# Attention stage: the previous image's last products with v ahead of an image's first scores, the first image's k moved by ScalarE, another order in the last half image

## The chip, the cores and the metric

The kernel runs on one core of a Trainium2 chip. The metric is the device time of one execution in microseconds (us), as the median of several runs. The core has a matrix engine (TensorE, PE in the profile), VectorE (DVE), ScalarE (ACT), GpSimd (POOL) and SyncE (SP), which work side by side and wait for one another by semaphores. SP, ACT and POOL also issue DMAs. Matrix products land in PSUM, everything else is in SBUF.

## The reference

The input x is an array of 8 images with 384 channels and 32 x 32 pixels, in float32. Four layers follow one another, each of the form x + f(GroupNorm(x)).

- Layer 0 is the one that is changed here. For each of q, k and v: a depthwise 3x3 convolution, a batch norm (mean and variance over all images and pixels), gelu, and a 384 x 384 product over the channels. Then attention over the 1024 pixels of an image with 8 heads of 48 channels, an output projection w_out, and a batch norm.
- Layer 1 is a mixture of 4 experts (the best 2 by a gate), layer 2 a 7x7 depthwise convolution, layer 3 three branches with convolutions and small MLPs that are fused.

```
y = dwconv3x3(x)                       # for q, k and v, each with own weights
y = gelu(batch_norm(y))                # statistics over batch and pixels
q, k, v = pw @ y                       # 384 x 384, per image
att = softmax(q.T @ k / sqrt(48)) @ v  # per image and head, 1024 x 1024
out = batch_norm(w_out @ att)
```

## The kernel before, in words

**Convolution stage.** The 384 channels are three tiles `ct` of 128. A loop runs over 36 groups n = (ct, v, u): channel tile, which of q, k, v (0, 1, 2), and a quarter u of the rows. A group is a set of banded matmuls (L373) into a PSUM tile `ps` (2 buffers). Its weights come by a DMA on ACT's queue (L319) and are spread by `spread0(n)` into `wx` (3 buffers), one half by ACT (L327), one by POOL (L328), two groups ahead. ACT copies `ps` into `o` (L406), a tile for four groups with 2 buffers. When a set of four is complete, `results()` on DVE transposes an image's share (L342), takes batch norm statistics (L164) and SP stores it to `raw[v][b]` in HBM (L344); these calls are spread over the next four groups, and the last set's follow after the loop. When all of q or k is there, `coefs0(v)` makes the batch norm's scale and shift: DVE (L230, L158), a power on POOL (L159), and DVE again (L232 to L234). `y0` loads image 0's q or k back (on SP), and `gelu0(v)` applies scale, shift and gelu on ACT (L224). The order on PE, ACT and DVE is the written order (`manual_schedule(engines=ORDERED)`); POOL and SP are ordered by a scheduler.

**Attention stage**, `attention(False)`. The same three engines run in written order. The list `todo` has (b, h, pair, g): image, half of its query pixels, pair of heads (4 pairs), and half of its key pixels. So an image has 16 steps, numbered j. For each step

- `scores` makes four score tiles of 128 x 1024 (L597), and ACT takes exp of each (`e`, L604, 8 buffers);
- `attend` multiplies the e of the step before with v (L616) into a tile `av` (2 buffers in PSUM). Row sums come out of the same product, as vT has columns of ones;
- after the second g, `norm` shuffles the sums (L630), takes the reciprocal (L632) and multiplies (L634, or L638 for the fourth pair), and checks the sums against overflow (L644, L647).

The first three pairs write rows of `att` directly; the fourth goes to `att3` and from there by three POOL DMAs (L640) into every fourth row of `att`. `project_out(b, h)` then makes z = w_out @ att (L655), and DVE copies z and takes moments (L659 to L663); POOL stores z (L668).

At j = 0 of an image come `project_k` and `project_q` (L505), both through `spread`: for each of three tiles a product into PSUM, an ACT affine that writes all 128 rows (L224), and 32-row moves by DVE that gather the fourth pair (L523; for q L525 with a factor). Then follow scores, the attend of the previous image's last step, and `project_v` (L550):

```
es = scores(*t)
complete = attend(*last) if last else None
if j == 0:
    project_v(b)
```

The PSUM pool `sc` has three tiles of two banks (`two_banks`), which k, q, v, scores and project_out all take in turn. For the first image, `begun` is true: gelu of k and q is done by `gelu0`, and that of v (`activate(b, 2)`) follows project_q.

**After the last step**: `attend`, `norm`, the check's minimum (`ok`, L712, L713), one matmul with ones that adds it up (L717), `shift_needed` (L718), and `project_out(7, 1)`. `shift_needed` is loaded as a value (L726), and an `If` (L727) would repeat attention with a shift of the maximum; it is not taken in these runs. The next stage begins with `bn_coefs(zst, ...)` on DVE (L230).

Of the kernel before, what the change touches and what calls it, by code (L numbers as in the profile page):

```python
# [11 lines left out]
FP = mybir.dt.float32  # L12
# [6 lines left out]
P = 128  # L19
# [71 lines left out]
def conv_mixer_kernel(ctx: ExitStack, tc: tile.TileContext, a: dict, out: bass.AP):  # L91
# [171 lines left out]
    with (  # L263
        tc.tile_pool(name="cw", bufs=1) as cw,
        tc.tile_pool(name="cxa", bufs=1) as cxa,
        tc.tile_pool(name="co", bufs=2, reuse_waits="tile") as co,
        tc.manual_schedule(engines=ORDERED),
    ):
        bn_gb = load(cw, "bn_gb", nc.scalar)
        stats = cw.tile([P, 9, 2 * B, 6], FP, name="stats")  # L270
# [19 lines left out]
        with tc.tile_pool(name="cy", bufs=3, reuse_waits="tile") as cy, tc.tile_pool(  # L290
# [72 lines left out]
            for n, (ct, v, u) in enumerate(groups):  # L363
                if u == 0:

                    o = co.tile([P, B, H, 32], FP, tag="o", name="o")
                w = weights0.pop(n).rearrange("p r t w -> p r (t w)")
                ps = cps.tile([P, 4, 2, B, H], FP, tag="ps", name="ps")
                for cc in range(2):
                    for k in range(3):  # L370
                        for e, d, i in product(range(2), repeat=3):
                            r = slice(64 * i, 64 * i + 64)
                            nc.tensor.matmul(  # L373
                                ps[64 * d : 64 * d + 64, 2 * i + e, cc],
                                lhsT=w[r, 12 * cc + 6 * e + 3 * d + k, :],
                                rhs=xt0s[ct][r, 16 * d + 8 * e + 2 * u + cc, :, k : k + H],
                                start=k == 0, stop=k == 2,
                            )
# [27 lines left out]
                nc.scalar.copy(  # L406
                    o.rearrange("p b h (i c) -> p i c (b h)", i=4)[:, :, 2 * u : 2 * u + 2],
                    ps.rearrange("p i c b h -> p i c (b h)"),
                )
# [26 lines left out]
    def attention(shifted):  # L436
# [3 lines left out]
        with tc.tile_pool(name="aw", reuse_waits="tile", bufs=1) as aw, tc.tile_pool(  # L440
# [68 lines left out]
                        )  # L509
                return ps.rearrange("p h n -> p (h n)")  # L510

            def spread(w, y, o, own):


                for t in range(NC):
                    ps = project(w, t, y)
                    to = [[(0, None)], [(32, 1), (64, 2)], [(96, None)]][t]
                    affine(o[:, t, :], ps, own[:, 0:1] if own is not None else 1.0, 0.0)
                    moves = [(o[64:96, t, :], 32, 2)]
                    moves += [(o[p : p + 32, NP - 1, :], 64, i) for p, i in to]  # L520
                    for d, p, i in moves:
                        if own is None or i is None:
                            nc.vector.tensor_copy(d, ps[p : p + 32, :])  # L523
                        else:
                            nc.vector.tensor_scalar(  # L525
                                d, ps[p : p + 32, :], own[p : p + 32, i : i + 1], None, ALU.mult
                            )

            def project_k(b):
                kT = kTs[b] = ay.tile([P, NP, N], FP, tag="kT", name="kT", bufs=1)  # L530
                if not shifted:
                    return spread(pw_k, ys[b][1], kT, None)
                for pair in range(NP):
                    affine(kT[:, pair, :], project(pw_k, pair, ys[b][1]), 1.0, ones_row)

# [69 lines left out]
                    es.append(e)  # L605
                return es

            def attend(b, h, pair, g, es):

                if g == 0:  # L610
                    attend.av = avp.tile([P, HF], FP, tag="av", name="av")
# [1 line left out]
                for e, m in zip(es, range(g * GM, (g + 1) * GM)):  # L613
                    for s in range(2):
# [2 lines left out]
                            av[64 * s : 64 * s + 64, :], lhsT=vT[:, m, c0 : c0 + 64],  # L617
                            rhs=e[:, s, :], start=m == 0, stop=m == N // P - 1,
                        )
                if g == NG - 1:  # L620
                    return lambda: norm(b, h, pair, av)

            def norm(b, h, pair, av):

                if pair == 0:
# [5 lines left out]
                inv = ay.tile([P, HF], FP, tag="inv", name="inv")  # L631
                nc.vector.reciprocal(inv, sm)  # L632
                if pair < NC:
                    nc.vector.tensor_mul(atts[b, h][:, pair, :], av, inv)  # L634
                else:

                    att3 = ay.tile([P, HF], FP, tag="att3", name="att3")
                    nc.vector.tensor_mul(att3, av, inv)  # L638
                    for t in range(NC):
                        nc.gpsimd.dma_start(out=atts[b, h][3::4, t, :], in_=att3[t::4, :])  # L640
                if not shifted:

                    i = (b * 2 + h) * NP + pair
                    nc.vector.scalar_tensor_tensor(  # L644
# [1 line left out]
                    )  # L646
                    nc.vector.tensor_reduce(chk[:, i : i + 1], inv, AX.X, ALU.min)  # L647

            def project_out(b, h):
                att, x, k = atts.pop((b, h)), xs.pop((b, h)), 2 * b + h  # L650
                z = ay.tile([P, NC, HF], FP, tag="z", name="z", bufs=1 if shifted else 2)
                for oc in range(NC):
                    ps = two_banks()[:, 0, :]
                    for t in range(NC):
                        nc.tensor.matmul(  # L655
                            ps, lhsT=w_out[:, t, oc * P : (oc + 1) * P], rhs=att[:, t, :],
                            start=t == 0, stop=t == NC - 1,
                        )
                    nc.vector.tensor_copy(z[:, oc, :], ps)  # L659
                    nc.vector.bn_stats(zst[:, oc, k, :], z[:, oc, :])  # L660
                    nc.vector.bn_aggr(mvz[:, :, oc, k], zst[:, oc, k, :])
                    nc.vector.bn_aggr(mvxh[:, :, oc, k], xst[:, oc, k, :])
                    nc.vector.scalar_tensor_tensor(  # L663
                        out=x[:, oc, :], in0=z[:, oc, :], scalar=mvz[:, 0, oc, k : k + 1],
                        in1=x[:, oc, :], op0=ALU.subtract, op1=ALU.mult,
                        accum_out=zx[:, oc, k : k + 1],
                    )
                nc.gpsimd.dma_start(out=zraw[b][:, :, h * HF : (h + 1) * HF], in_=z)  # L668
# [41 lines left out]
            if not shifted:  # L710
                ok = small.tile([P, 1], FP, tag="ok1", name="ok1")
# [6 lines left out]
                nc.vector.tensor_scalar(shift_needed, ps[:1, :1], P - 0.5, None, ALU.is_lt)  # L718
            project_out(B - 1, 1)

    with tc.manual_schedule(engines=ORDERED):
        attention(False)
# [1054 lines left out]
def lay_out(inp):  # L1777
# [37 lines left out]
        o[f"pw_{v}"] = tiles_b(w.reshape(C, NC, P))  # L1815
    o["pw_v"] = tiles_b(f["L0_conv_pw_v"].T)
    w = f["L0_conv_w_out"].T[:, ORDER_A].reshape(NP, 32, 3, C)
    w = np.concatenate([w[:NC], w[NC].swapaxes(0, 1)[:, :, None]], 2)
    o["w_out"] = np.moveaxis(w.reshape(NC, P, C), 0, 1)

# [96 lines left out]
```

## Time and profile before

| what | value |
| --- | --- |
| median of 3 runs | 3377.09 us (3377.02 to 3389.05) |
| the profiled execution: its time, its span | 3390.1 us, 3388.4 us |
| mean granted TensorE clock | 0.972 |
| PE busy | 3156.8 us, 93% of the span |
| DVE, ACT, POOL busy | 1609.1, 1333.1, 238.0 us |
| convolution stage, last groups | 229 to 290 us: PE busy 44.63 of 61 |
| attention, first image's start | 290 to 360 us: PE busy 59.32 of 70 |
| attention, steady | 360 to 1744 us: PE busy 1365.27 of 1384 |
| attention, end | 1744 to 1772 us: PE busy 18.06 of 28 |
| into the next layer | 1772 to 1795 us: PE busy 7.57 of 23 |

A row of the timeline has the start in us, the busy time in us, the engine and line, the operation with out<-in, the tile's shape, the number of instructions that it joins, and in brackets the idle time of the engine before it with what ended it. Rows that are joined (x36) have the busy time of all. A row of the chain has the start, its length and what it was; "issue" is time in which nothing that the profile shows was waited for. A matmul in float32 appears as two PE instructions for most tiles here (L655 has nine products and x18).

### The profile page before, as it was taken

How to read it: one execution, taken by the hardware profiler on the slowest of the kernel's cores; microseconds unless marked ns; L12 is line 12 of the kernel's file. 1: busy time of each engine (PE TensorE's matmuls, PEld its weight loads, DVE VectorE, ACT ScalarE, POOL GpSimd, SP SyncE). 2: the span in 40 equal slices, each digit the busy share in tenths (PEclk: the TensorE clock that was granted, in tenths of full speed). 3: DMA queues.
4: the chain of work that ended last, by engine and by line, in shares of the span. 5: the costliest groups of instructions: out<-in, count | busy, mean ns of one | idle time of the engine just before them, and what ended most of it. 6: DMA issues, size and time to landing. Idle time of an engine off the chain costs nothing.

```text
span 3388.4 us, 40142 instructions
## 1 busy us (share of the span) xinstructions
PE 3156.8 (93%) x16784; PEld 1467.1 (43%) x16784; DVE 1609.1 (47%) x2199; ACT 1333.1 (39%) x1375; POOL 238.0 (7%) x398
## 2 busy tenths in 40 slices
PE   5887999999999999999988999999999998985989
PEld 4763333343434343433323444444444444654544
DVE  6997344444444444444453554343343342356164
ACT  4874453535354444445424302121121111556520
POOL 3321000000000000000000000000000000110300
PEclk9998999999999999999998999999999998997989
DMA  5886011010101110110017313121121111666766
GB/s 211 287 290 242 20 40 58 28 70 22 66 32 59 40 59 22 56 42 19 21 38 266 101 50 99 47 79 42 56 79 42 44 39 35 238 211 220 229 203 200
DMA packets 97862, 339.06 MB, mean 100 GB/s; under 512 B 14440, under 2 KB 17088, under 8 KB 93320
## 3 DMA queue, kind: packets, MB, share of 16 engines
q1 hardware_dynamic: 73672, 266.95, 23.4%
q10 hardware_dynamic: 13776, 36.90, 3.5%
q0 software_dynamic: 10224, 32.56, 2.8%
q8 instruction: 134, 2.20, 0.3%
q14 instruction: 56, 0.46, 0.0%
HBM read 237.18 MB, written 102.32 MB: 100 GB/s over the span
## 4 chain that ended last, share of the span: by engine, by line
PE 68%; issue 10%; DVE 9%; DMA 7%; ACT 4%; POOL 1%; ACTq 0%; SPq 0%; POOLq 0%; DVEq 0%
PE av L616 14%; PE sc L597 13%; PE ph L815 9%; PE y L1028 9%; PE sc L505 7%; PE sc L550 4%; PE sc L655 4%; DVE stats L164 2%; DVE y L342 2%; PE ps L1369 2%; DMA cb<-cfmem 1%; DMA w<-in_w 1%; PE po L1747 1%; PE po L1750 1%; PE po L1758 1%
## 5 line engine op out<-in xcount | busy, mean ns | idle before, releaser
L604 ACT ACTIVATE e<-sc 128x1024 f32<-128x1024 f32 x512 | 484.2, 1030 | 583.0 <-PE sc L597 582.8
L1028 PE MATMUL y<-hs,w 128*128 128x512 f32 x1152 | 521.5, 594 | 10.2 <-DVE hs L1013 10.2
L815 PE MATMUL ph<-xn,w 128*128 128x512 f32 x1152 | 526.7, 596 | 2.0 <-ACT xn L224 2.0
L597 PE MATMUL sc<-qT,kT 64*128 64x512 f32 x2048 | 481.8, 607 | 22.1 <-DVE qT L523 15.4
L616 PE MATMUL av<-e,vT 128*64 128x512 f32 x2048 | 468.9, 600 | 0.0
L819 ACT ACTIVATE hs<-ph,b 128x512 f32<-128x512 f32 x192 | 131.6, 685 | 642.3 <-PE ph L815 634.6
L1028 PEld LDWEIGHTS y<-hs,w 128*128 128x128 f32 x1152 | 217.1, 190 | 286.4 <-issue 258.6
L815 PEld LDWEIGHTS ph<-xn,w 128*128 128x128 f32 x1152 | 216.9, 191 | 270.3 <-issue 260.7
L597 PEld LDWEIGHTS sc<-qT,kT 64*128 64x128 f32 x2048 | 186.5, 186 | 309.9 <-issue 232.0
L1013 DVE TENSOR_TENSOR hs<-hs,cb 128x512 f32<-128x512 f32 x192 | 130.0, 686 | 376.1 <-ACT hs L819 370.0
L616 PEld LDWEIGHTS av<-e,vT 128*64 128x64 f32 x2048 | 135.9, 137 | 318.6 <-issue 318.6
L505 PE MATMUL sc<-y,pw 128*128 128x512 f32 x576 | 253.9, 602 | 13.6 <-issue 7.3
L373 PE MATMUL ps<-xt,wx 64*64 64x256 f32 x3456 | 199.8, 389 | 47.1 <-DVE xt L309 19.8
L632 DVE RECIPROCAL inv<-sm 128x512 f32<-128x512 f32 x64 | 214.6, 3353 | 2.2
L630 DVE LOAD_MASK_SELECT sm<-av x64 | 0.9, 14 | 417.1 <-PE av L616 417.1
L373 PEld LDWEIGHTS ps<-xt,wx 64*64 64x64 f32 x3456 | 153.1, 138 | 92.7 <-issue 44.6
L1369 PE MATMUL ps<-xt,wx 64*64 64x256 f32 x2688 | 161.1, 399 | 21.5 <-ACT wx L1116 16.5
L505 PEld LDWEIGHTS sc<-y,pw 128*128 128x128 f32 x576 | 110.3, 193 | 156.6 <-issue 147.1
L1018 DVE SCALAR_TENSOR_TENSOR r<-cb,b,r 128x512 f32<-128x512 f32 x192 | 134.2, 745 | 73.0 <-DMA cb<-cfmem 69.8
L406 ACT COPY o<-ps 128x2048 f32<-128x2048 f32 x36 | 135.1, 3759 | 55.1 <-PE ps L373 33.1
L1116 ACT ACTIVATE wx<-w,parity 128x448 f32<-128x448 f32 (+2 forms) x192 | 108.3, 617 | 105.4 <-POOL w L1103 31.7
L1369 PEld LDWEIGHTS ps<-xt,wx 64*64 64x64 f32 x2688 | 106.5, 140 | 75.0 <-ACT wx L1116 19.7
(299 smaller groups left out, 2895.7 us busy)
## 6 DMA issues: line engine op xcount, KB each, us to landing
raw<-y SPq DMA_DIRECT2D x72, 512.0 KB
y<-raw SPq DMA_DIRECT2D x24, 1536.0 KB
xr<-in_x SPq DMA_DIRECT2D x42, 512.0 KB
cb<-cfmem SPq DMA_DIRECT2D x64, 256.0 KB
w<-in_w ACTq DMA_DIRECT2D x36, 384.0 KB
xn<-in_x SPq DMA_DIRECT2D x24, 512.0 KB
x<-in_x SPq DMA_DIRECT2D x16, 768.0 KB
z<-z POOLq DMA_DIRECT2D x16, 768.0 KB, 4.3
```

Source lines behind the costliest of these rows:

```text
L373: nc.tensor.matmul(ps[64 * d : 64 * d + 64, 2 * i + e, cc], lhsT=w[r, 12 * cc + 6 * e + 3 * d + k, :], rhs=xt0s[ct][r, 16 * d + 8 * e + 2 ...
L406: nc.scalar.copy(o.rearrange("p b h (i c) -> p i c (b h)", i=4)[:, :, 2 * u : 2 * u + 2], ps.rearrange("p i c b h -> p i c (b h)"),)
L505: nc.tensor.matmul(ps[:, h, :], lhsT=w[:, ct, pair, :], rhs=y[:, ct, h * HF : (h + 1) * HF], start=ct == 0, stop=ct == NC - 1,)
L550: nc.tensor.matmul(ps[:, m, :C], lhsT=y[:, ct, (m0 + m) * P : (m0 + m + 1) * P], rhs=pw_v[:, ct, :], start=ct == 0, stop=ct == NC - 1,)
L597: nc.tensor.matmul(sc[:, s, :], lhsT=kTs[b][r, pair, m * P : (m + 1) * P], rhs=qTs[b][r, pair, h * HF : (h + 1) * HF], start=True, stop=True,)
L604: nc.scalar.activation(e, sc, AF.Exp, scale=1.0 if shifted else HD**-0.5)
L616: nc.tensor.matmul(av[64 * s : 64 * s + 64, :], lhsT=vT[:, m, c0 : c0 + 64], rhs=e[:, s, :], start=m == 0, stop=m == N // P - 1,)
L632: nc.vector.reciprocal(inv, sm)
L655: nc.tensor.matmul(ps, lhsT=w_out[:, t, oc * P : (oc + 1) * P], rhs=att[:, t, :], start=t == 0, stop=t == NC - 1,)
L815: nc.tensor.matmul(ph, lhsT=w1[:, e, ct, dc * P : (dc + 1) * P], rhs=xn[:, ct, :], start=ct == 0, stop=ct == NC - 1,)
L1028: nc.tensor.matmul(py[oc], lhsT=w2[:, e, dc, oc * P : (oc + 1) * P], rhs=hs, start=k == 0, stop=k == len(TODO) - 1,)
L1369: nc.tensor.matmul(ps[64 * d : 64 * d + 64, 2 * i + e, c % 2], lhsT=w[r, d * K7 + k, :], rhs=xts[ct][r, 16 * d + 8 * e + c, :, k : k + H], ...
```

## The change

1. In the convolution stage POOL too runs in written order.
2. The load of `y0` moves from u = 3 to u = 1; `coefs0(v - 1)` and `gelu0` stand ahead of the group's copy of `ps` instead of behind it.
3. For image 0, the 32-row moves of k are ACT copies instead of DVE copies (`spread(..., act=b == 0)`), seven of them.
4. At j = 0 of images 1 to 7, `attend` of the previous image's last step stands ahead of the scores, so that the order on PE is k, q, attend, scores, v. For image 0, `project_v` stands ahead of the first scores: k, q, v, scores.
5. In the last half image (7, h = 1) the pairs go in the order 3, 0, 1, 2. `att3` of this half is not scattered into `att`; the output projection uses it as a fourth tile, with its own weights `w_last` (four tiles, prepared by the host's layout, loaded by SP at step 1 of image 7 into the buffer of `y0`). After the last attend, the products for att3, pair 0 and pair 1 stand on PE, then those for pair 2, which wait for `norm`. ACT copies z, DVE takes the moments from PSUM, and the check follows the last norm's product. The matmul with ones writes to an `av` tile.

```diff
-        tc.manual_schedule(engines=ORDERED),
+        tc.manual_schedule(engines=ORDERED | {mybir.EngineType.Pool}),
...
+                if ct == NC - 1 and v > 0 and u == 1:
+                    y0 = pp0.tile([P, NC, N], FP, tag=f"y{v - 1}", name="y0")
+                    nc.sync.dma_start(out=y0, in_=raw[v - 1][0])
+                    ys0[v - 1] = y0
+                if ct == NC - 1 and v > 0 and u == 3:
+                    coefs0(v - 1)
+                if m == 8 and u in (1, 3):
+                    gelu0(u // 2)
                 nc.scalar.copy(
...
                 if u == 3:
                     last, last_o = (ct, v), o
-                    if ct == NC - 1 and v > 0:
-                        coefs0(v - 1)
-                        y0 = pp0.tile([P, NC, N], FP, tag=f"y{v - 1}", name="y0")
-                        nc.sync.dma_start(out=y0, in_=raw[v - 1][0])
-                        ys0[v - 1] = y0
-                if m == 8 and u in (1, 3):
-                    gelu0(u // 2)
...
-                        if own is None or i is None:
+                        if act:
+                            nc.scalar.copy(d, ps[p : p + 32, :])
+                        elif own is None or i is None:
...
-                    return spread(pw_k, ys[b][1], kT, None)
+                    return spread(pw_k, ys[b][1], kT, None, b == 0)
...
-                    for t in range(NC):
-                        nc.gpsimd.dma_start(out=atts[b, h][3::4, t, :], in_=att3[t::4, :])
-                if not shifted:
+                    if (b, h) == (B - 1, 1):
+                        atts[NC] = att3
+                    else:
+                        for t in range(NC):
+                            nc.gpsimd.dma_start(out=atts[b, h][3::4, t, :], in_=att3[t::4, :])
...
+            def project_tile(ps, att, oc, t, w):
+                nc.tensor.matmul(
+                    ps, lhsT=w[:, t, oc * P : (oc + 1) * P], rhs=att,
+                    start=t == (0 if w is w_out else NC), stop=t == NC - 1,
+                )
...
             todo = [
                 (b, h, pair, g)
-                for b in range(B) for h in range(2) for pair in range(NP) for g in range(NG)
+                for b in range(B) for h in range(2)
+                for pair in (range(NP) if (b, h) != (B - 1, 1) else (NP - 1, *range(NC)))
+                for g in range(NG)
             ]
...
+                complete = None
+                if j == 0:
+                    if last:
+                        complete = attend(*last)
+                    if begun:
+                        project_v(b)
                 es = scores(*t)
-                complete = attend(*last) if last else None
+                if j > 0:
+                    complete = attend(*last)
+                if (b, j) == (B - 1, 1):
+
+                    y = pp0.tile([P, NC, N], FP, tag="y0", name="w_last", bufs=1)
+                    w_last = y.rearrange("p c n -> p (c n)")[:, : NP * C]
+                    w_last = w_last.rearrange("p (t c) -> p t c", c=C)
+                    nc.sync.dma_start(out=w_last, in_=a["w_last"])
                 if j == 0:
-                    project_v(b)
+                    if not begun:
+                        project_v(b)
...
-            attend(*last)()
-
+            b, h = B - 1, 1
+            k = 2 * b + h
+            av_last = attend(*last, keep=True)
+            att, x = atts.pop((b, h)), xs.pop((b, h))
+            z = ay.tile([P, NC, HF], FP, tag="z", name="z", bufs=1 if shifted else 2)
+            outs = [two_banks()[:, 0, :] for _ in range(NC)]
+            att3 = atts.pop(NC)
+            for t in (NC, *range(NC - 1)):
+                for oc in range(NC):
+                    project_tile(outs[oc], att3 if t == NC else att[:, t, :], oc, t, w_last)
+            for oc in range(NC):
+                half_moments_x(oc, k)
+            check_sums = norm(b, h, NC - 1, av_last, check=False, att=att)
+            for oc in range(NC):
+                project_tile(outs[oc], att[:, NC - 1, :], oc, NC - 1, w_last)
+                nc.scalar.copy(z[:, oc, :], outs[oc])
+            nc.gpsimd.dma_start(out=zraw[b][:, :, h * HF : (h + 1) * HF], in_=z)
             if not shifted:
+                check_sums()
                 ok = small.tile([P, 1], FP, tag="ok1", name="ok1")
...
-                ps = two_banks()[:, 0, :]
+                ps = avp.tile([P, HF], FP, tag="av", name="av")
...
-            project_out(B - 1, 1)
+            for oc in range(NC):
+                moments(outs[oc], x, oc, k, of_x=False)
+                if oc == 0 and not shifted:
+                    nc.vector.tensor_scalar(shift_needed, ps[:1, :1], P - 0.5, None, ALU.is_lt)
```

`moments` holds what `project_out` did for each third (statistics of z and the product with x), and `half_moments_x` the one aggregate of x in it.

More of the change, by code (lines that the diff above doesn't have):

```diff
@@ L510, in project, with spread @@
                 return ps.rearrange("p h n -> p (h n)")
-            def spread(w, y, o, own):
+            def spread(w, y, o, own, act=False):
                 for t in range(NC):
@@ L606, in scores, with attend @@
                 return es
-            def attend(b, h, pair, g, es):
+            def attend(b, h, pair, g, es, keep=False):
                 if g == 0:
@@ L619, in attend, with norm @@
                         )
+                if keep:
+                    return av
                 if g == NG - 1:
                     return lambda: norm(b, h, pair, av)
-            def norm(b, h, pair, av):
-                if pair == 0:
+            def norm(b, h, pair, av, check=True, att=None):
+                if att is None and (b, h) not in xs:
                     x = xs[b, h] = ay.tile([P, NC, HF], FP, tag="x", name="x", bufs=1)
@@ L633, in norm @@
                 if pair < NC:
-                    nc.vector.tensor_mul(atts[b, h][:, pair, :], av, inv)
+                    att = atts[b, h] if att is None else att
+                    nc.vector.tensor_mul(att[:, pair, :], av, inv)
                 else:
@@ L638, in norm, with check_sums @@
                     nc.vector.tensor_mul(att3, av, inv)
-                    for t in range(NC):
-                        nc.gpsimd.dma_start(out=atts[b, h][3::4, t, :], in_=att3[t::4, :])
-                if not shifted:
+                    if (b, h) == (B - 1, 1):
[3 more added lines that the diff above has]
+                            nc.gpsimd.dma_start(out=atts[b, h][3::4, t, :], in_=att3[t::4, :])
+                def check_sums():
                     i = (b * 2 + h) * NP + pair
@@ L647, in norm @@
                     nc.vector.tensor_reduce(chk[:, i : i + 1], inv, AX.X, ALU.min)
+                if not shifted:
+                    if not check:
+                        return check_sums
+                    check_sums()
             def project_out(b, h):
@@ L654, in project_out, with half_moments_x, moments @@
                     for t in range(NC):
[L655 to L658, printed above, removed]
+                        project_tile(ps, att[:, t, :], oc, t, w_out)
                     nc.vector.tensor_copy(z[:, oc, :], ps)
[L660 to L668, printed above, removed]
+                    moments(z[:, oc, :], x, oc, k)
+                nc.gpsimd.dma_start(out=zraw[b][:, :, h * HF : (h + 1) * HF], in_=z)
+            def project_tile(ps, att, oc, t, w):
[3 more added lines that the diff above has]
+                )
+            def half_moments_x(oc, k):
+                nc.vector.bn_aggr(mvxh[:, :, oc, k], xst[:, oc, k, :])
+            def moments(z, x, oc, k, of_x=True):
+                nc.vector.bn_stats(zst[:, oc, k, :], z)
+                nc.vector.bn_aggr(mvz[:, :, oc, k], zst[:, oc, k, :])
+                if of_x:
+                    half_moments_x(oc, k)
+                nc.vector.scalar_tensor_tensor(
+                    out=x[:, oc, :], in0=z, scalar=mvz[:, 0, oc, k : k + 1],
+                    in1=x[:, oc, :], op0=ALU.subtract, op1=ALU.mult,
+                    accum_out=zx[:, oc, k : k + 1],
+                )
             todo = [
                 (b, h, pair, g)
-                for b in range(B) for h in range(2) for pair in range(NP) for g in range(NG)
+                for b in range(B) for h in range(2)
+                for pair in (range(NP) if (b, h) != (B - 1, 1) else (NP - 1, *range(NC)))
+                for g in range(NG)
             ]
@@ L707, in attention @@
                     project_out(b, 0)
-            attend(*last)()
+            b, h = B - 1, 1
[9 more added lines that the diff above has]
+            for oc in range(NC):
+                half_moments_x(oc, k)
+            check_sums = norm(b, h, NC - 1, av_last, check=False, att=att)
[3 more added lines that the diff above has]
+            nc.gpsimd.dma_start(out=zraw[b][:, :, h * HF : (h + 1) * HF], in_=z)
             if not shifted:
+                check_sums()
                 ok = small.tile([P, 1], FP, tag="ok1", name="ok1")
@@ L715, in attention @@
                 nc.gpsimd.memset(ones_col, 1.0)
-                ps = two_banks()[:, 0, :]
+                ps = avp.tile([P, HF], FP, tag="av", name="av")
                 nc.tensor.matmul(ps[:1, :1], lhsT=ok, rhs=ones_col, start=True, stop=True)
-                nc.vector.tensor_scalar(shift_needed, ps[:1, :1], P - 0.5, None, ALU.is_lt)
-            project_out(B - 1, 1)
+            for oc in range(NC):
+                moments(outs[oc], x, oc, k, of_x=False)
+                if oc == 0 and not shifted:
+                    nc.vector.tensor_scalar(shift_needed, ps[:1, :1], P - 0.5, None, ALU.is_lt)
     with tc.manual_schedule(engines=ORDERED):
@@ L1817, in lay_out @@
     w = f["L0_conv_w_out"].T[:, ORDER_A].reshape(NP, 32, 3, C)
+    wl = np.pad(w, ((0, 0), (0, 0), (0, 1), (0, 0)))
+    o["w_last"] = np.moveaxis(wl.reshape(NP, P, C), 0, 1)
     w = np.concatenate([w[:NC], w[NC].swapaxes(0, 1)[:, :, None]], 2)
```

## The prediction

> **What bounds the kernel now.** I read the page's chain that ended last, then that chain in order of time, then the timeline at the joints of the attention stage. The page says who sets the end:
>
> ```profile
> PE 68%; issue 10%; DVE 9%; DMA 7%; ACT 4%; POOL 1%; ACTq 0%; SPq 0%; POOLq 0%; DVEq 0%
> ```
>
> TensorE carries the end, so an edit is worth what it takes out of PE's waits. In the windows view PE is busy 1365.27 us of the 1384 from 360 to 1744 us: inside attention little can be won, and it has to come from the joints. The chain in order of time (start us, us, what) shows one, the start of image 2:
>
> ```profile
> 659.00 31.11 PE sc L505 x72
> ...
> 690.14 1.12 ACT qT L224
> ...
> 691.28 1.28 DVE qT L525
> ...
> 692.58 1.24 DVE qT L523
> ...
> 693.95 1.99 PE sc L597 x8
> 695.93 3.58 PE av L616 x16
> 699.52 15.68 PE sc L550 x48
> ```
>
> The products for k and q end at 690.11. Two score tiles run at once; the third needs the PSUM tile that q's last moves (ACT, DVE, DVE) still read, so PE waits until 693.95. Only then come the previous image's last products with v (L616) and project_v (L550). From 690.11 to 699.52 is 9.41 us. The steady pattern does the same work in 3.63 + 3.58 = 7.21 us:
>
> ```profile
> 358.81 3.63 PE sc L597 x16
> 362.45 3.58 PE av L616 x16
> ```
>
> Images 1 and 3 lose more. The timeline of image 3 (start, us, engine and line; in brackets idle before) has, after the same wait,
>
> ```profile
> 875.27 2.46 PE L597 MATMUL sc<-qT,kT 64*128 64x512 f32 x8 [1.93 <-DVE qT L523]
> 877.66 4.83 PE L616 MATMUL av<-e,vT 128*64 128x512 f32 x16
> ```
>
> where image 2 has 1.99 and 3.65. From the first score (871.36) to project_v (882.42) it takes 11.06 us; the granted clock of the window around it is 0.97, of image 2's 1.00.
>
> At the first image DVE and ACT hold PE. The timeline around 285 to 315 us:
>
> ```profile
> 283.47 0.16 DVE L234 TENSOR_TENSOR bn_t<-bn_gb,bn_t 128x3 f32<-128x3 f32 x1
> 288.77 3.48 ACT L224 ACTIVATE y<-y,bn_t,bn_s 128x1024 f32<-128x1024 f32 x3
> 288.99 1.25 DVE L342 STREAM_TRANSPOSE y<-o 128x1024 f32<-128x1024 f32 x1 [5.36 <-ACT o L406]
> 307.61 2.86 ACT L224 ACTIVATE kT<-sc 128x1024 f32<-128x1024 f32 x3 [15.36 <-DVE y L342]
> 311.96 6.17 DVE L523 COPY kT<-sc 32x1024 f32<-32x1024 f32 x5
> 314.51 18.55 PE L505 MATMUL sc<-y,pw 128*128 128x512 f32 x36 [7.31 <-issue]
> ```
>
> k's products are done at 307.2 and wait: ACT may write kT only after DVE's last transpose (306.27 + 1.23 = 307.50), and DVE's k moves come after its statistics, two of them (2.45 us) before the first PSUM tile is free and q can start at 314.51. At the other end of the stage:
>
> ```profile
> 1751.87 3.35 DVE L632 RECIPROCAL inv<-sm 128x512 f32<-128x512 f32 x1
> 1758.38 10.81 PE L655 MATMUL sc<-att,w_out 128*128 128x512 f32 x18 [0.21 <-DMA att<-att]
> 1770.22 0.74 POOL L668 DMA_DIRECT2D z<-z  x1 [12.17 <-DVE z L659]
> 1775.83 1.48 DVE L230 BATCH_NORM_AGGREGATE bn_mv<-zst 128x2 f32<-128x96 f32 x3 [4.17 <-DVEq L727]
> ```
>
> The last products with v end at 1751.06; all of norm, the att3 DMAs, the check and 18 passes of the output projection (10.81 us, 7.92 at its usual rate in the chain) follow one another.
>
> **Part 1, images 1 to 7: attend ahead of the scores.** The exps that attend reads belong to the previous image and ran during its last half and 31 us of k and q, so it can start at 690.11 and run 3.58 us to 693.69. By then q's moves are done (693.80), and the scores follow without the wait: 7.21 us to project_v. The new wait to look for is the third score tile, due at 693.7 + 1.8 = 695.5, after 693.80: none. The exps start 3.6 us later, but their next reader comes only after project_v's 15.68 us, and four exps at 0.97 us with the 1.28 us table load need 5.2. Saved: 9.41 - 7.21 = 2.20 in five images (their stretches are 9.40 or 9.41), 3.85 in images 1 and 3 (11.06): 11.0 + 7.7 = **18.7 us**. If the half-rate spells moved elsewhere instead of going, seven times 2.2 = 15.4 stay; if a third of the wait stayed in new places, 12.
>
> On those spells the row speaks first: after a wait of 1.93 us PE ran slow in two of seven images, after 7.31 us for some 6 us (weight loads 0.855 apart, then 0.43). [...]
>
> **Part 2, the first image.** Several small moves. Pool in written order puts wx(32) and wx(33) ahead of coefs0(0)'s power, which waits 17.82 us for DVE (L159); PE's idle of 9.60 us at 260.10 shrinks by about 6.7. This is worth nothing by itself: the o copy of group 31 already ends at 259.34, DVE's results run without a gap from 259.37 to 280.40, and coefs0(1) is done at 283.63 either way. The y0 loads and raw stores keep their places on SP but for one exchange. gelu0(1) then stands ahead of the last o copy on ACT: k's products start near 285 instead of 290, which only lets them wait longer, while the copy, 3.6 us, ends at 283.7 + 3.5 + 3.7 = 290.9 instead of 288.96. Behind it queue DVE's eight transposes: **1.95 us late**, the last one at 309.45. From there k's first tile takes three ACT instructions (one affine, two copies). The trace has no ACT copy of 32x1024 from PSUM; the nearest row is ACT's 128x1024 move of the same tile, 2.86/3 = 0.95 us apart, the upper end is DVE's 6.17/5 = 1.23. I take 0.95, since it is the same engine and length: q can start at 312.4 + 0.1 instead of 314.51, 2.0 us sooner (with 1.23: 1.2). All seven copies cost ACT 6.7 us; q's first tile, slow as now, covers them. DVE loses them (8.6 us), and its coefs0(2) stands before them already.
>
> [...] The rows of this case, ACT 0.95 against DVE 1.23, decide for ACT.
>
> q takes 18.55 us as now, to 331.0. gelu of v follows q's last ACT move (1.0 us) as in the trace (333.11, 334.12 + 3.49): 332.1 to 335.6. project_v now comes first and needs it; PE starts at 333.3, meets the third part at 335.6, and with 15.0 to 16.1 us for the rest (chain 15.68, timeline here 16.81) ends near 351.2. Scores take 3.63 and some 0.5 for the exp table: 355.4 against 358.81 now. Gained: **3.4 us**. Bounds: -2 (the late transposes stay and ACT wins nothing) to 8 (the gelu exposed nowhere, no slow spell).
>
> **Part 3, the last half image.** Pair 3 goes first, so att3 needs no DMA; the projection has twelve matmuls in place of nine (PE shows each as two, 24 for 18). The first nine, for att3 and pairs 0 and 1, take 18 x 0.44 = 7.92 us from 1751.06 to 1759.0, beside norm, whose product is ready at 1751.1 + 0.76 + 3.39 + 0.73 = 1756.0. The last three, 2.64 us, end at 1761.7 instead of 1769.2. ACT copies z (three times some 0.7), and the store is issued near 1762.5 instead of 1770.22. DVE's moments no longer copy: 0.69 + 0.18 + 0.83 = 1.75 us with gaps for each third, from about 1760.8 to 1766.1 instead of 1771.66; then its 4.17 us of branch: 1770.3 against 1775.83. The check's matmul, in an av tile, stands on PE after the last products and delays nobody there. Gained: **5.4 us**. Bounds: 3 (moments wait for the copies, the branch for the later check) to 7. w_last, 786 KB, is queued on SP in a stretch where DMA's share is 0.12, and its reader comes some 57 us later: nothing. In its place three POOL DMAs go.
>
> Sum: 18.7 + 3.4 + 5.4 = **27.5 us**. The profiled execution took 3390.1 us, 1.7 beyond its span, and would take 3362.6. The median of the runs is 3377.09, 13.0 lower; no term above rests on that difference, so I set 3377.09 - 27.5 = 3349.6, say **3350**.
>
> **Rivals.**
> - *Only the fixed waits go* (0.15). The slow spells reappear, 15.4; the late transposes eat what the k copies give, 0; the tail gives 1 to 3 because the later check holds the branch. Sum 16 to 18, around 3361: within 0.5% (16.9 us, about what a measurement of this kernel can tell from no change). For it: project_v at the first image has a new wait of 2.3 us before it.
> - *It doesn't do what it says* (0.05): the third score tile or the exps find a new wait behind attend, half of part 1 stays, 9 + 2 + 4 = 15, 3362. Against it: the PSUM tile's readers end at 693.80, before the need.
> - *Slower* (0.05): a fuller PE is granted less clock. Attention has 1384 us; a clock lower by 27.5/1384 = 2.0% takes all gain, 3.2% would add 17 us: about 3394. Against it: the fullest windows show 1.00, and the emptiest ones 0.55 (1772 to 1795) and 0.82 (1744 to 1772).
>
> **How the numbers follow.** The forecast has 0.75. Unknown costs reach from 12 - 2 + 3 = 13 to 20 + 8 + 7 = 35 us: 3342 to 3364. The runs of before lie between 3377.02 and 3389.05, and a median can land off its lower end, so the range is 3341 to 3366. Faster by over 0.5% means under 3360.2: forecast and the better half of the first rival's edge, 0.78; same 0.17; slower 0.05.
>
> **What would show it.** Right: in the chain L505 is followed by L616 x16, L597 x16, L550 with no ACT or DVE between, seven times; gelu0 before the last o copy, DVE's transposes starting near 291, q near 312.5; L550 before the first L597; at the tail PE idle of 0 between the last L616 and L655, DVE resuming 19 us after it. Wrong: a wait on av, vT or e at a joint; slow weight loads there; q later than 314.5; a clock under 0.97 overall. The forecast falls if attention from first to last score is not shorter by some 20 us.

## The result, and the profile after

The kernel after takes 3356.07 us (median of 5 runs, 3355.34 to 3361.0), the kernel before 3381.12 beside it (5 runs): a ratio of 0.9925, with a 95% interval of 0.9912 to 0.9938. In a later group of runs the ratio was 0.9934 (0.9915 to 0.9953). The gain is 25.05 us by these medians; forecast were 27.5. The profiled execution took 3360.26 us, with a span of 3358.5 and a granted clock of 0.976 (before 0.972).

The page's chain by engine hardly moves, and it could not show more, as 25 us are 0.7% of the span:

```profile
PE 67%; issue 12%; DVE 9%; DMA 7%; ACT 4%; POOL 1%; SPq 0%; ACTq 0%; another core or an unknown queue 0%; POOLq 0%; DVEq 0%
```

The joint at image 2 in the chain in order of time (start us, us, what):

```profile
654.19 31.10 PE sc L506 x72
685.28 3.58 PE av L619 x16
688.87 1.08 PE sc L600 x4
...
690.02 0.83 ACT L607
...
691.31 1.03 ACT e L607
...
692.39 1.13 PE sc L600 x4
693.52 15.68 PE sc L553 x48
```

The attend now follows the products for k and q without a wait, and the scores follow it. But the scores stop again: three tiles run, and the fourth waits until the first exp has freed its PSUM tile. That exp stands behind a load of its table on ScalarE (L607), and the load begins only when the first score tile is done. From q's end to project_v it takes 693.52 - 685.28 = 8.24 us, where before had 9.40 or 11.05 and the forecast 7.21. The slow spells of images 1 and 3 are gone.

The first image in the timeline (idle time of the engine in brackets):

```profile
285.63 0.16 DVE L234 TENSOR_TENSOR bn_t<-bn_gb,bn_t 128x3 f32<-128x3 f32 x1
285.83 3.50 ACT L224 ACTIVATE y<-y,bn_t,bn_s 128x1024 f32<-128x1024 f32 x3 [7.50 <-DVE bn_t L234]
292.88 1.25 DVE L342 STREAM_TRANSPOSE y<-o 128x1024 f32<-128x1024 f32 x1 [7.08 <-ACT o L414]
311.50 1.02 ACT L224 ACTIVATE kT<-sc 128x1024 f32<-128x1024 f32 x1 [18.65 <-DVE y L342]
312.55 2.02 ACT L524 COPY kT<-sc 32x1024 f32<-32x1024 f32 x2
314.62 18.32 PE L506 MATMUL sc<-y,pw 128*128 128x512 f32 x36 [9.08 <-ACT kT L524]
```

q starts where it started before (314.51), but everything here is 2.16 us later from the first line on. Measured from k's coefficients (L234), q starts after 28.99 us instead of 31.04.

The end of the stage:

```profile
1737.40 10.57 PE L675 MATMUL sc<-att,w_last 128*128 128x512 f32 x24
1738.29 3.35 DVE L637 RECIPROCAL inv<-sm 128x512 f32<-128x512 f32 x1
1748.89 0.73 POOL L766 DMA_DIRECT2D z<-z  x1 [41.95 <-DVE shift_needed L779]
1755.26 1.48 DVE L230 BATCH_NORM_AGGREGATE bn_mv<-zst 128x2 f32<-128x96 f32 x3 [3.34 <-DVEq L787]
```

The output projection begins with the last attend's end and covers norm. DVE comes to the next layer 17.9 us after that end, instead of 24.8.

### The profile page after: what moved, and what is told of

Read it like the earlier page. It is cut to its first block, busy times and chain, and to the rows that moved or that the text cites. A ratio compares the mean times of both kernels' runs of the same rounds, so it can differ in the third digit from the quotient of the medians.

```text
span 3358.5 us, 40148 instructions
## 1 busy us (share of the span) xinstructions
PE 3150.9 (94%) x16790; PEld 1473.7 (44%) x16790; DVE 1599.0 (48%) x2189; ACT 1340.9 (40%) x1385; POOL 238.1 (7%) x395
## 4 chain that ended last, share of the span: by engine, by line
PE 67%; issue 12%; DVE 9%; DMA 7%; ACT 4%; POOL 1%; SPq 0%; ACTq 0%; another core or an unknown queue 0%; POOLq 0%; DVEq 0%
PE av L619 13%; PE sc L600 12%; PE ph L875 9%; PE y L1088 9%; PE sc L506 7%; PE sc L553 4%; PE sc L675 3%; PE ps L1429 2%; DVE stats L164 2%; DVE y L342 2%; DMA w<-in_w 1%; PE po L1810 1%; PE po L1807 1%; PE po L1818 1%; DVE xt L309 1%
## 5 line engine op out<-in xcount | busy, mean ns | idle before, releaser
L607 ACT ACTIVATE e<-sc 128x1024 f32<-128x1024 f32 x512 | 483.1, 1030 | 545.8 <-PE sc L600 545.5
L373 PEld LDWEIGHTS ps<-xt,wx 64*64 64x64 f32 x3456 | 161.3, 139 | 82.8 <-issue 50.6
L1078 DVE SCALAR_TENSOR_TENSOR r<-cb,b,r 128x512 f32<-128x512 f32 x192 | 134.3, 745 | 69.0 <-DMA cb<-cfmem 67.7
L1429 PEld LDWEIGHTS ps<-xt,wx 64*64 64x64 f32 x2688 | 106.0, 138 | 70.1 <-ACT wx L1176 17.2
```

The lines of the kernel that those rows point to most:

```text
L373: nc.tensor.matmul(ps[64 * d : 64 * d + 64, 2 * i + e, cc], lhsT=w[r, 12 * cc + 6 * e + 3 * d + k, :], rhs=xt0s[ct][r, 16 * d + 8 * e + 2 ...
L607: nc.scalar.activation(e, sc, AF.Exp, scale=1.0 if shifted else HD**-0.5)
L1078: nc.vector.scalar_tensor_tensor(out=out[oc], in0=cb[e], scalar=b2[:, oc, e : e + 1], in1=out[oc], op0=ALU.mult, op1=ALU.add,)
L1429: nc.tensor.matmul(ps[64 * d : 64 * d + 64, 2 * i + e, c % 2], lhsT=w[r, d * K7 + k, :], rhs=xts[ct][r, 16 * d + 8 * e + c, :, k : k + H], ...
```

## The experiments

For all kernels one point and three stretches were read from the trace: when k's coefficients are ready (start of L234 in coefs0(1)), the time from there to the first attend on PE, from the first attend to DVE's first instruction of the next layer, and from there to the first y product of the experts. All in us.

| run | k's coefficients at | to the first attend | to the next layer | to its first y |
| --- | --- | --- | --- | --- |
| before | 283.47 | 78.91 | 1413.45 | 150.55 |
| joint_alone | 280.71 | 78.72 | 1400.82 | 149.25 |
| start_alone | 282.87 | 74.00 | 1412.37 | 148.77 |
| end_alone | 282.89 | 78.41 | 1408.42 | 147.68 |
| after | 285.63 | 74.75 | 1394.88 | 147.81 |
| after_again | 286.30 | 73.51 | 1395.12 | 147.62 |
| v_behind | 284.54 | 76.09 | 1394.94 | 148.00 |
| k_by_dve | 285.39 | 77.86 | 1394.87 | 148.19 |
| pool_free | 284.99 | 75.45 | 1395.16 | 148.07 |
| early_table | 281.67 | 73.80 | 1380.64 | 147.99 |
| gelu_behind | 281.43 | 65.06 | 1395.09 | 147.79 |
| early_gelu | 287.72 | 64.73 | 1380.71 | 148.09 |
| early_gelu_again | 279.80 | 64.80 | 1380.95 | 148.32 |
| gelu_v_first | 285.73 | 67.80 | 1380.94 | 148.26 |

The first column scatters over 8 us, even between equal kernels (early_gelu twice, 287.72 and 279.80); the others repeat within about 1.3 us where the stretch has the same code, the last one within 1.8 (before and start_alone, 150.55 and 148.77). So single runs differ by several us before attention begins, and edits of 2 us are read from the stretches, not from the medians.

**The three parts alone.**

```diff
 joint_alone (before, and)
-                es = scores(*t)
-                complete = attend(*last) if last else None
+                complete = None
+                if j == 0 and last:
+                    complete = attend(*last)
+                es = scores(*t)
+                if j > 0:
+                    complete = attend(*last)
```

> The kernel before, with only attend moved ahead of the scores at j = 0 of images 1 to 7. Theory from the trace of after: each joint keeps one wait, of the fourth score tile for the first exp, which stands behind the exp table load; five joints fall from 9.4 to 8.2 us and two from 11.06 to 8.2, so attention is shorter by some 11.5 us. Rival, the prediction: 7.2 us a joint, 18.7 us. Rival: joints differ without the other parts and the two slow ones stay slow, 5 us.

Ratio 0.9958 (0.9944 to 0.9972), 14 us by the ratio; the stretch to the next layer is 12.6 us shorter, and all joints have 8.23 us. From the first attend's start to the last one's end it is 11.6 us (1388.7 to 1377.1). The other 1.0 lies behind that end: with the same code, the output projection took 10.81 us in the profiled run of before and 9.77 here (9.74 in start_alone). The first theory holds, the forecast's 18.7 does not.

end_alone is before with the edits for the last half image: the order of pairs, att3, w_last, and all that follows the loop.

```diff
 end_alone (before, and)
+                for pair in (range(NP) if (b, h) != (B - 1, 1) else (NP - 1, *range(NC)))
...
+                    if (b, h) == (B - 1, 1):
+                        atts[NC] = att3
...
+                if (b, j) == (B - 1, 1):
+                    ...  # load of w_last
...
-            attend(*last)()
+            av_last = attend(*last, keep=True)
+            ...  # products by w_last, norm, z by ScalarE, moments, as in the change
```

> The kernel before, with only part 3 (the last half image and what follows it). From the last attend's end to DVE's first instruction of the next layer after has 17.9 us against 24.8: 6.9 us gained. If the end owes this to itself, this run shows 6 to 7.5 us, and the next layer's first y products another 2 to 3. Rival, the prediction: 5.4. Rival: part of it comes from the earlier parts, under 4.

Ratio 0.9984 (0.9975 to 0.9993). The last attend ends at 1751.56 and DVE resumes at 1769.72: 18.16 us instead of 24.77, so 6.6 are gained at this place; against joint_alone and start_alone, whose old end takes 23.7 us, it is 5.5. The whole stretch is only 5.0 shorter, because in this run three joints took 11.05 us instead of two in before.

start_alone is before with all of the diff's edits in the convolution stage, k by ScalarE, and project_v ahead of the first scores.

```diff
 start_alone (before, and the convolution stage as in the change, and)
-                    return spread(pw_k, ys[b][1], kT, None)
+                    return spread(pw_k, ys[b][1], kT, None, b == 0)
...
+                if j == 0 and begun:
+                    project_v(b)
                 es = scores(*t)
...
-                    project_v(b)
+                    if not begun:
+                        project_v(b)
```

> The kernel before, with only the first image's part: POOL in written order, coefs0 and gelu0 ahead of the o copy, k by ScalarE, project_v ahead of the first scores. In after q starts at 314.6 as before and the first attend ends 2.0 us sooner: theory 2 us, within what the runs can tell. Rival, the prediction: 3.4, with q 2.0 sooner. Rival: the late transposes make it slower, up to 2 us.

Ratio 0.9988 (0.9976 to 1.0): by the medians it can't be told from no change. The stretch to the first attend is 4.9 us shorter, more than both the theory and the forecast had.

**What holds the first image.** In each of these, one edit of after is undone.

```diff
 gelu_behind (after, and)
-                if m == 8 and u in (1, 3):
-                    gelu0(u // 2)
                 nc.scalar.copy(
                     o.rearrange("p b h (i c) -> p i c (b h)", i=4)[:, :, 2 * u : 2 * u + 2],
                     ps.rearrange("p i c b h -> p i c (b h)"),
                 )
+                if m == 8 and u in (1, 3):
+                    gelu0(u // 2)
```

> The kernel after, with gelu0 put back behind the group's copy of ps. In after the last o copy waits on ScalarE behind the gelu of k, and DVE stands idle 7.1 us before the last transposes. Theory: this is the step that ate the start's gain. The copy now runs as soon as PE is done, DVE's transposes start about 6 us sooner, k's products end near 306 and q follows without a gap: 6 to 8 us faster than after. Rival, the diff's order: k's products are late by the copy's 3.6 us and nothing is won, 0 to 2 slower. Rival: the stores of y to HBM hold the transposes (four buffers), 2 to 3 us won.

Ratio 0.9891 (0.9874 to 0.9908). The timeline of this kernel:

```profile
281.43 0.16 DVE L234 TENSOR_TENSOR bn_t<-bn_gb,bn_t 128x3 f32<-128x3 f32 x1
281.55 1.25 DVE L342 STREAM_TRANSPOSE y<-o 128x1024 f32<-128x1024 f32 x1
300.18 1.02 ACT L224 ACTIVATE kT<-sc 128x1024 f32<-128x1024 f32 x1 [15.04 <-DVE y L342]
303.30 15.72 PE L506 MATMUL sc<-y,pw 128*128 128x512 f32 x36 [1.68 <-ACT kT L524]
```

DVE goes from k's coefficients into the last transposes without a wait (7.08 us in after), q follows k after 1.68 us instead of 9.08, and its 36 products take 15.72 us against 18.32. The first attend comes 9.7 us sooner than in after and 8.5 sooner than in after_again, more than the 6 to 8 expected. The one edit of the diff that put gelu0 ahead of the copy cost this much.

```diff
 k_by_dve (after, and)
-                    return spread(pw_k, ys[b][1], kT, None, b == 0)
+                    return spread(pw_k, ys[b][1], kT, None)
```

> The kernel after, with the first image's k moves by VectorE again (seven 32x1024 copies). DVE has its last statistics and coefs0(2) after the last transpose, some 3.2 us, before the first move. Theory: q starts 3.7 us later than in after, against the last transpose, and the run is 3 to 4 us slower. Rival: q's start is hidden by something else, no difference. In the prediction the move was worth 2.0 to 4 us.

Ratio 0.9922 (0.9908 to 0.9935), not to be told from after's by time. In the trace q starts at 318.17, 32.78 us after k's coefficients instead of 28.99, and the first attend 3.1 and 4.4 us later than in the two runs of after. The move of k to ScalarE is worth that. ACT's 32x1024 copies took 1.00 us each, DVE's 1.22.

```diff
 v_behind (after, and)
-                    if begun:
-                        project_v(b)
                 es = scores(*t)
...
-                    if not begun:
-                        project_v(b)
+                    project_v(b)
```

> The kernel after, with project_v behind the first image's first scores again. From k's coefficients to the first attend after takes 74.8 us, before 78.9. If k by ScalarE gives 2 of the 4.1 and the order of v gives the rest, this one takes 76.8 and the run is 2 us slower, within what the runs can tell. Rival: all of it comes from k's moves, no difference.

Ratio 0.9945 (0.9928 to 0.9962). The first attend comes 1.3 to 2.6 us later than in the two runs of after: the order of project_v and the first scores is worth that.

```diff
 pool_free (after, and)
-        tc.manual_schedule(engines=ORDERED | {mybir.EngineType.Pool}),
+        tc.manual_schedule(engines=ORDERED),
```

> The kernel after, with POOL ordered by the scheduler again in the convolution stage. The prediction: PE's idle time near 260 us comes back (about 6 us), and nothing changes at the end, since DVE's chain through the results is the limit: within 1 us of after. Rival: the late weights delay the last groups' copies and with them q, 3 to 6 us slower.

Ratio 0.9917 (0.9904 to 0.993), and 75.45 us to the first attend, 0.7 and 1.9 more than the two runs of after, which differ by 1.2 themselves. PE has an idle time of 10.74 us at 261.65 again, and of those at most 2 reach the first attend; the rest is hidden, as was forecast, and whether the 2 are real these runs can't tell. That POOL's order is worth so little holds with gelu0 ahead of the copy. In pool_free PE ends its last group at 289.01, and the copy starts right then (289.07), so there gelu0 holds it no longer. By these rows the gain of gelu_behind needs PE to be as early as in after (282.08), and with it POOL's order; no run has POOL free and gelu0 behind the copy, so this is not shown.

**The table load.**

```diff
 early_table (after, and)
+            exp_t = aw.tile([P, 3], FP, name="exp_t")
...
+            def load_exp():
+                if not shifted:
+                    nc.scalar.activation(exp_t, own, AF.Exp)
...
                     if begun:
                         activate(b, 2)
+                    load_exp()
...
                         activate(b + 1, 1)
+                        load_exp()
                     project_out(b, 0)
```

> The kernel after, with one exp of a 128x3 tile on ScalarE after q's last move of every image and after the gelu in the middle of images 0 to 6, so that the exp table is loaded while PE is still at the products. If the wait of 1.03 us at each joint is the table load, it goes at 7 joints and at 7 places in the middle: 14 us faster than after, about 3342. Rival: the fourth tile waits for the first exp itself, load or not: the joint stays at 8.2 and the run at 3356. Rival: PSUM readers of q are the limit, half of it, 7 us.

3345.12 us, ratio 0.9876 (0.9861 to 0.9891). The chain at image 1:

```profile
468.10 31.10 PE sc L507 x72
499.20 3.58 PE av L624 x16
502.78 3.63 PE sc L601 x16
506.42 15.68 PE sc L554 x48
```

From q's end to project_v 7.22 us: the forecast's joint, once the load no longer waits for a score tile. The stretch to the next layer is 14.2 us shorter than in after, 1.02 us at each of 14 places. ScalarE at this joint, in after and then in early_table:

```profile
509.86 1.28 ACT L607 ACT_TABLE_LOAD   x1 [3.58 <-PE sc L600]
511.15 3.77 ACT L607 ACTIVATE e<-sc 128x1024 f32<-128x1024 f32 x4
...
500.37 1.28 ACT L614 ACT_TABLE_LOAD   x1
501.66 0.20 ACT L614 ACTIVATE exp_t<-own 128x3 f32<-128x3 f32 x1
503.95 3.77 ACT L608 ACTIVATE e<-sc 128x1024 f32<-128x1024 f32 x4 [2.08 <-PE sc L601]
```

The first theory holds.

**Both together, and one step more.** early_gelu has the edits of early_table and of gelu_behind; early_gelu_again is the same kernel, after_again is the kernel after.

> The kernel after with both the early exp table (7 joints, 7 middles, the first image) and gelu0 behind the copy of ps. The two are in different stretches of time: the sum of both, 11 + 6 = 17 us faster than after if the second theory holds, about 3339; 11, about 3345, if it does not.

3339.31 us, ratio 0.9849 (0.9835 to 0.9862). That it meets the expected 3339 is luck, as 17 us were expected under after and the stretches are 24.2 shorter than in after (10.0 to the first attend, 14.2 behind it); before was slower in this group of runs, 3389.17.

> The kernel after once more, on the chip of the runs beside it. By its own ratio, 0.9925 of before. It also shows how far the point at which k's coefficients are ready (283.5 us before, 285.6 in after) moves from run to run: if the 2 us are the change's, it is near 285.6 again; if they are scatter of the stores and loads in the convolution stage, anywhere between 280.7 and 287.7.

3365.79 us, ratio 0.9934; k's coefficients at 286.30, and 73.51 us to the first attend.

> The best kernel so far (early exp table, gelu0 behind the copy) beside after on one chip. Its parts gave 14 and 10 us in the traces: 24 us under after, a ratio of 0.985 to before.

3339.43 us, ratio 0.9862 (0.9843 to 0.9882). That is 26.4 us under after_again, which ran beside it: the version to keep.

```diff
 gelu_v_first (early_gelu, and)
-                    if not begun:
-                        activate(b, 2)
+                    activate(b, 2)
                     project_q(b)
-                    if begun:
-                        activate(b, 2)
```

> The best kernel so far, and the first image's gelu of v ahead of q's moves on ScalarE, so that project_v has not to wait 2.3 us for it. If v has landed in time (q's first move can wait until about 318), PE goes from q to v without a gap and the first attend comes 2.5 to 3.5 us sooner. Rival: v lands later, near 322, q's moves then hold project_v's PSUM tile, and nothing is won.

3337.47 us, ratio 0.9859 (0.984 to 0.9878), no different from early_gelu. The timeline shows the rival:

```profile
321.05 3.50 ACT L224 ACTIVATE y<-y,bn_t,bn_s 128x1024 f32<-128x1024 f32 x3 [6.35 <-DMA y<-raw]
328.34 18.19 PE L554 MATMUL sc<-pw_v,y 128*128 128x384 f32 x48 [5.07 <-ACT qT L224]
```

ScalarE stands 6.35 us before v's data, with q's moves queued behind it, and PE then waits 5.07 us for those. The first attend is 3.0 us later than in early_gelu.

## Why the prediction was right, and where its sum was not

The time, the direction and the size came out: 25 us gained, 27.5 forecast. The terms did not come out as well as the sum.

- **Part 1, the joints: 18.7 forecast, 11.6 measured** from the first attend to the last. The wait for q's moves went as described, and so did the slow spells; both were read rightly. The step that failed is the sentence that no new wait follows. It looked at the third score tile, whose PSUM tile q's moves free in time, and it set the exps aside because their reader comes only after project_v. But exps have a second client: the fourth score tile needs the PSUM tile of the first. The price was in the trace of before, in the chain of the middle of images 0 to 6, where the same four tiles have a table load and an exp between them (447.29 and 448.58 us) and take 4.66 us, 1.03 more than elsewhere (the rows stand below). Seven joints at 1.02 are the 7.1 us that are missing: 18.7 - 7.1 = 11.6. early_table took the load away and found the forecast's 7.2 us.

```profile
446.13 1.08 PE sc L597 x4
...
447.29 0.83 ACT L604
...
448.58 1.03 ACT e L604
...
449.66 1.13 PE sc L597 x4
```

- **Part 2, the first image: 3.4 forecast, 4.2 measured** from k's coefficients (78.91 to 74.75; 4.9 and 5.4 in start_alone and after_again). The order of steps was right: q 2.05 us sooner (2.0 forecast), project_v's end 67.75 us after the coefficients (351.2 - 283.47 = 67.7 forecast). The late transposes were named, with 1.95 us; their real price against the other order is 8.5 to 9.7, because without the gelu the copy would have been earlier than in before, PE being ahead there: PE's last group ends 5.2 us before k's coefficients in gelu_behind, 3.6 before them in after, and 0.3 behind them in before. So the gain that the order of POOL made for PE was spent by the place of gelu0. In the profiled run 2.2 us of the part were lost again, since the coefficients came that much later. The prediction has DVE's results from 259.37 to 280.40 without a gap, but DVE waits there 1.19 us for a store, at 275.46; in after it waits 2.01 us, and its results start at 260.72. Those 0.82 and 1.35 us are the 2.2. Whether the change has a share in that stays open: the point scatters from 279.8 to 287.7 us, 280.7 to 283.5 in the three runs with the old order of that stage and 279.8 to 287.7 in the others.
- **Part 3, the end: 5.4 forecast, 6.6 to 6.9 measured.** ACT's z copies took 0.58 us instead of 0.7, DVE's moments ended 0.5 us sooner after the attend than reckoned, and the wait at the branch was 3.34 us instead of 4.17. Another 1.0 of the 6.9 is the slow output projection of before's profiled run; against the other runs with the old end the gain is 5.5 to 6.0. The load of w_last was issued 151 us ahead of its reader (1586.1 and 1737.4), not 57; it cost nothing, as forecast.
- **Not in the sum:** the first y product of the experts comes 2.7 us sooner after DVE's first instruction than in before. 1.3 to 1.8 of that also appear in joint_alone and start_alone, which have the old end, so they belong to a slow spell of PE in before's run (12.26 us for 24 products of L815 where the others take 10.57). About 1 us is left for the end; it was not separated further.

Together: 11.6 + 4.2 + 6.9 + 2.7 = 25.4 us, less 2.2 in the profiled pair for the later coefficients. That pair differs by 29.9 us in its spans; the rest arose in the later layers, whose code is the same, and is no part of the change. That the sum comes so near to 27.5 is partly luck: part 1 fell 7.1 us short, the other terms came out 5.0 larger, and 2.3 to 2.9 of these are slow spells of before's profiled run. The three parts alone gain 14, 5 and 4 us by their ratios.

Of the signs that the prediction named, "no ACT or DVE between" failed at all seven joints, where an exp and its table load stand. The one on the time from first to last score decides nothing: it fell by 33.9 us (1410.45 to 1376.56), but project_v ahead of the first scores takes some 22 out of it by itself (1388.14 in start_alone).

The first rival ("only the fixed waits go") was wrong in its reason, as the slow spells did go. The second was half right: a new wait behind attend was there, with the exps, at 7 of 18.7 us instead of half. A lower granted clock did not come: 0.976 against 0.972.

On the slow spells it was right to follow the trace of before. There two of seven joints (images 1 and 3) took 11.05 us instead of 9.40, all after a wait of 1.93 us; in start_alone and end_alone, whose joints have the same code, it was images 2 and 6, and images 1, 3 and 7. In after and joint_alone, where PE waits 0.74 us at a joint, none was slow. The granted clock in the traces of before and after is 1.00 or 0.50, and in each of the two all its stretches at 0.50 begin on one grid of 3.41 us. At image 1 of before it is 1.00 from 508.02 to 511.43, where PE waits its 1.93 us and is busy for 1.48, and 0.50 from 511.43 to 514.84. Of the seven joints of before, four have their wait across a border of that grid, with up to 1.61 us of it on one side, and none was slow; three have it inside one cell, and two were slow (the third, image 7, has its wait begin 0.03 us behind a border). What lowers the clock these traces do not show.

## What to carry to other kernels

When a wait is taken out of a chain, follow every buffer that the next instructions need, not only the one that was waited for: here the fourth tile of a pool of three was a client of the exp that emptied the first, and the joints took 8.24 us, against 7.22 with the exp's table load moved. A table load that stands before an activation can wait together with it, as the 1.28 us load did here; a 3-column exp of 0.20 us, placed behind q's last move or the gelu, where ScalarE had idle time, took the load out of the way, 1.02 us at each of 14 places. And an edit that lets an engine start early is spent if the next instruction of another queue stands behind something that is not yet ready: gelu0 ahead of the copy cost 8.5 to 9.7 us here.

## What the runs showed of the hardware

The ACT_TABLE_LOAD took 1.28 us and here waited for the same product as the exp behind it: in after ScalarE was idle from 506.27 to 509.86 us and loaded only then. With a 3-column exp of 0.2 us ahead, the load ran while PE was at other products, and each of 14 places became 1.02 us shorter. In after the exp starts 0.01 us after the load's end (511.14 and 511.15). Where ScalarE works up to the load, in before, an exp ends at 435.94, the load runs from 435.95 to 437.24 and a gelu starts at 437.25: 1.31 us from the one to the other.

Moves of k's 32 and 128 partitions from PSUM took ScalarE in after nearly the same time: 1.00 us for a copy of 32 x 1024 and 1.02 for an affine of 128 x 1024. VectorE's copy of 32 x 1024 took 1.22 us in before.
